# First-layer attention units: the reciprocals of the softmax sums fetched from HBM as a tenth row beside the nine taps' weights

## The chip, the core and the metric

The kernel runs on one core of one Trainium2 chip. The core has five engines that work side by side, each through its own instructions in order: TensorE (PE, matmuls; PEld is its loading of weights), VectorE (DVE), ScalarE (ACT), GpSimd (POOL) and SyncE (SP), whose queue issues the DMAs here. The metric is device time in microseconds (us) for one execution; the time of a kernel is the median of its runs.

## The reference, cut to what matters

The network has four layers; the change is in the first, an attention of 8 heads of 64 channels over 64 x 64 positions, for two images. Each position attends to its own 3 x 3 neighbourhood (nine "local" keys) and to 256 pooled keys, with one softmax over both; learned weights are added to the local part after the softmax.

```python
attn_local = jnp.einsum('bhnd,bhndk->bhnk', q_scaled, k_local)
...
attn = jax.nn.softmax(jnp.concatenate([attn_local, attn_pool], axis=-1), axis=-1)
a_local, a_pool = (attn[..., :ll], attn[..., ll:])
lt = jnp.einsum('bhnd,hdk->bhnk', q_norm, learnable_tokens) + learnable_bias[None] + a_local
x_local = jnp.einsum('bhnk,bhndk->bhnd', lt, v_local)
x_pool = jnp.einsum('bhnp,bhpd->bhnd', a_pool, v_pool)
xo = (x_local + x_pool).transpose(0, 2, 1, 3).reshape(B, N, C)
```

So the output at a position needs, for each head, ten numbers spread over the head's 64 channels: the reciprocal of the softmax sum, by which the pooled part is multiplied, and nine local weights, by which the nine shifted copies of the values are multiplied.

## The kernel before

Class `Local` computes this layer. The work is cut into 16 units per image: four chunks of 128 channels (two heads) by four pieces of 1024 positions. Channels lie on the 128 partitions. `run` goes through iterations; in each, several units are in the making at different stages, written as generators that take turns (`in_turn`): the projections and norms of later units, the tap products and sums of the next unit (`tap_products`, `tap_sums`), the attention of this one (`attend`), and the weighing of the one before (`weigh`). The framework schedules the result: it fixes an order of instructions for each engine ahead of the run, which is not always the order in which they are written, and adds the waits between engines. So what stands next to what on an engine can change in places where the code was not touched.

The steps by line:

- `tap_products` (L2126, VectorE): for tap k of 9, queries times shifted keys, 128 x 1024, into one of three buffers (product k goes to buffer k mod 3). `tap_sums` (L2139, TensorE): sums these over the 64 channels of each head; two matmuls (one for each half of 512 positions) per tap, 18 per unit, each of 32 output rows, all into one bank "tap". ScalarE's exponential (L2154) of that bank is the tile `el`: rows 2k and 2k+1 of each group of 32 belong to tap k, and the rows from 18 on have weights of zero, so there `el` is exp(0) = 1.
- `attend`: scores against the pooled keys (L2171), exponentials (L2175), values (L2181) into `out`, GpSimd's additions of the exponentials (L2186), the softmax sums in the layout of `el` (L2193, L2197), their reciprocals (L2218) in `recip`. Then `el` is multiplied by `recip` and the learned part is added (L2221, L2222; it is zero in the rows from 18 on), and `el` is written to HBM as `rows` (L2225).
- `fetch_tap` (L2235): one row of `rows` is read back for each head and written to all of the head's 64 partitions; two DMAs fill one 128 x 1024 tap tile. There are three tap tiles, taken in turn.
- `weigh`: the reciprocals are spread over the partitions by two TensorE matmuls (L2248, two rows of `recip` by a matrix of zeros and ones, into two banks), and VectorE multiplies `out` by them (L2251). Then for each tap k: ScalarE copies the tap tile into two PSUM banks (L2258), VectorE multiplies the shifted values by them, back into the tap tile (L2261), GpSimd adds the tile to `out` (L2265), and the tile is free for the fetch of tap k + 3. At the end `out` is stored to HBM as `yd` (L2271), from where `output` (L1966) reads it for the last projection.

Other lines that stand between these on the engines: L133 (the projections' matmuls), L2036, L2043, L2064, L2078 (the norms' matmuls), L2050 to L2058 (small VectorE steps of the norms), L2086 (the norms' multiplication), L2099 (learned part), L2183 (copy of the values), L1983 (loads of projection weights).

PSUM banks called "mm" come from a pool of five, given out in turn in the order in which the code asks: whoever takes a bank waits for the last reader of the tile that stood in it five requests before. The banks of L2248 and of L2258 are taken from this pool, like those of L133, L2171 and L2181.

Of the kernel before, what the change touches and what calls it, by code (L numbers as in the profile page):

```python
# [11 lines left out]
ALU = mybir.AluOpType  # L12
# [3 lines left out]
P = 128  # L16
# [4 lines left out]
TB = 512  # L21
# [3 lines left out]
HD = 64  # L25
# [16 lines left out]
def bcast(ap, axis, n):  # L42

    a = ap.unsqueeze(axis)
    shape = list(a.shape)
    shape[axis] = n
    return a.to_broadcast(shape)
# [10 lines left out]
class General:  # L58
# [130 lines left out]
    def layer0(self, X, Y, sp_scale, tokT, d):  # L189
        tc, nc, vec = self.tc, self.nc, self.vec  # L190
        with tc.tile_pool(name="l0", bufs=1) as sp:
# [7 lines left out]
            with tc.tile_pool(name="l0b", bufs=2) as wp, \  # L199
                    tc.tile_pool(name="l0s", bufs=2, space=PSUM) as pps, \  # L200
                    tc.tile_pool(name="l0m", bufs=3, space=PSUM) as pp, \
                    tc.tile_pool(name="l0o", bufs=1, space=PSUM) as ppo:
                taps = wp.tile([18, 9, P], F32, name="taps", bufs=1)
                nc.sync.dma_start(taps, d["taps"])
                steps = []
                for cc in range(KC):
                    steps += self.local_chunk(X, Y, cc, xs, nmean, rstd, sp_scale, tokT, taps, d,
                                              wp, pps, pp, ppo)
                in_turn(steps[0][0]())
                for i, (_, attend) in enumerate(steps):  # L210
                    ahead = [steps[i + 1][0]()] if i + 1 < len(steps) else []
                    in_turn(attend(), *ahead)
# [63 lines left out]
    def local_chunk(self, X, Y, cc, xs, nmean, rstd, sp_scale, tokT, taps, d, wp, pps, pp, ppo):  # L276
# [137 lines left out]
        def attend(blk):  # L414
# [48 lines left out]
            nc.vector.tensor_tensor(Y[:, cc, blk * TB:(blk + 1) * TB], acc, psO, ALU.add)  # L463

        return [(lambda b=b: prepare(b), lambda b=b: attend(b)) for b in range(NB)]


# [1225 lines left out]
class Local:  # L1693
# [464 lines left out]
    def attend(self, u):  # L2158

        nc = self.nc  # L2160
        cc = u // self.UN
        qs, el = self.qs[u % 3], self.el[u]
        out = self.att()
        prob = {}
        self.out[u] = out
        heads = [slice(h * HD, (h + 1) * HD) for h in range(2)]

        def exponentials(j, k2):
            pS = [self.bank() for _ in range(2)]
            for h, c in enumerate(heads):  # L2170
                nc.tensor.matmul(pS[h], self.kp[c, cc, k2 * P:(k2 + 1) * P],  # L2171
                                 qs[c, j * TB:(j + 1) * TB], start=True, stop=True)
            prob[j, k2] = [self.prob() for _ in range(2)]
            for h in range(2):
                nc.scalar.activation(prob[j, k2][h], pS[h], AF.Exp)  # L2175

        def values(j):
            psO = self.bank()
            for k2 in range(2):
                for h, c in enumerate(heads):  # L2180
                    nc.tensor.matmul(psO[c, :], self.vp[:, k2, cc * P + h * HD:][:, :HD],  # L2181
                                     prob[j, k2][h], start=(k2 == 0), stop=(k2 == 1))
            nc.scalar.copy(out[:, j * TB:(j + 1) * TB], psO)  # L2183
            dst = prob[1, 1] if j else self.halves
            for h in range(2):
                nc.gpsimd.tensor_tensor(dst[h], prob[j, 0][h], prob[j, 1][h], ALU.add)  # L2186

        def sums():
            psD = self.bank()
            blocks = [slice(j * HD, (j + 1) * HD) for j in range(2)]  # L2190
            for h in range(2):
                for j, b in enumerate(blocks):
                    nc.tensor.matmul(psD[b, :], self.cst[:, C_EVEN + h:C_EVEN + h + HD],  # L2193
                                     (prob[1, 1] if j else self.halves)[h], start=(h == 0),
                                     stop=False)
            for b in blocks:
                nc.tensor.matmul(psD[b, :], self.cst[b, C_SD:C_SD + HD], el[b, :], start=False,  # L2197
                                 stop=True)
            return psD

        exponentials(0, 0)
        yield
        exponentials(0, 1)
        yield
        values(0)
        yield
        exponentials(1, 0)
        yield
        exponentials(1, 1)
        yield  # L2210
        values(1)
        yield
        yield
        psD = sums()

        for i in range(2):
            part = slice(i * TB // 2, (i + 1) * TB // 2)
            nc.vector.reciprocal(self.recip[:, part], psD[:, part])  # L2218
        yield
        el = self.el.pop(u)  # L2220
        nc.vector.tensor_tensor(el, el, self.recip, ALU.mult)  # L2221
        nc.vector.tensor_tensor(el, el, self.lt.pop(u), ALU.add)  # L2222
        self.spread = self.rows()
        for j in range(2):
            nc.sync.dma_start(self.spread[:, j * TB:(j + 1) * TB], el[j * HD:(j + 1) * HD, :])  # L2225
        self.fetch_tap(0)
        yield
        self.fetch_tap(1)
        yield

    def fetch_tap(self, k):

        at = 32 * (k % 2) + 2 * k
        for h in range(2):
            self.nc.sync.dma_start(self.taps[k % 3][h * HD:(h + 1) * HD, :],  # L2235
                                   bcast(self.spread[at + h], 0, HD))

    def weigh(self, u):

        nc = self.nc  # L2240
        cc, y0 = u // self.UN, u % self.UN * self.UY
        out, R = self.out.pop(u), self.recip
        self.fetch_tap(2)
        yield
        banks = [self.bank() for _ in range(2)]
        for j, ps in enumerate(banks):
            q = slice(64 * j, 64 * j + 2)
            nc.tensor.matmul(ps, self.cst[q, C_ROW:C_ROW + P], R[q, :], start=True, stop=True)  # L2248
        for j, ps in enumerate(banks):
            o = out[:, j * TB:(j + 1) * TB]  # L2250
            nc.vector.tensor_tensor(o, o, ps, ALU.mult)  # L2251
        for k in range(9):
            dy, dx = divmod(k, 3)
            parts = [self.taps[k % 3][:, j * TB:(j + 1) * TB] for j in range(2)]

            banks = [self.bank() for _ in range(2)]
            for ps, part in zip(banks, parts):
                nc.scalar.copy(ps, part)  # L2258
            for j, (ps, part) in enumerate(zip(banks, parts)):
                y = y0 + dy + j * self.UY // 2  # L2260
                nc.vector.tensor_tensor(  # L2261
                    part.rearrange("p (y x) -> p y x", x=W),
                    self.vx[:, y:y + self.UY // 2, dx:dx + W],
                    ps.rearrange("p (y x) -> p y x", x=W), ALU.mult)
            nc.gpsimd.tensor_tensor(out, out, self.taps[k % 3], ALU.add)  # L2265
            if k + 3 < 9:
                self.fetch_tap(k + 3)
            if k < 8:
                yield
        lo = u % self.UN * self.UT  # L2270
        nc.sync.dma_start(self.yd[:, cc, lo:lo + self.UT], out)  # L2271
        yield
# [161 lines left out]
```

## Time and profile before

| | us |
|---|---|
| median of 9 runs | 5500.97 |
| lowest, highest | 5495.19, 5508.07 |
| the profiled execution: time | 5499.75 |
| the profiled execution: span from first to last instruction | 5497.9 |
| loop of units, first image | about 346 to 1112 |
| loop of units, second image | about 3070 to 3836 |

In the 766 us of each loop, TensorE is busy for 745 us, VectorE for 529, GpSimd for 415, ScalarE for 376, and the mean granted clock is 0.99. The starts of L2248 in the first image are 361.68, 407.66, 453.52 and so on to 866.33, then 906.44, 946.11, 1000.73 and 1041.15: eleven equal steps, and then units in which less is projected and the output is computed beside them.

How to read it: "busy" is the time in which an engine executes; an engine that waits is idle. Each fp32 matmul of the code is two records of MATMUL in the profile. In a timeline line stand the start, the duration, the engine, the line of the code, the operation, output and input tiles (`late` is a tile from which `out`, `el`, `recip` and the exponentials are cut; `big` holds the keys, values, queries and two of the three tap tiles), shapes, and in brackets how long the engine had been idle and on what it waited last. A matmul's end is modelled, so the start of the next one tells better how long it held the engine.

### The profile page before, as it was taken

The numbers are of one execution on the slowest core, as the hardware profiler recorded it, in microseconds if no ns is written. First come the engines' busy times: TensorE is split into PE (matmuls) and PEld (weight loads), VectorE is DVE, ScalarE is ACT, GpSimd is POOL, SyncE is SP. The second block draws the span as 40 slices with busy tenths as digits, with TensorE's granted clock in tenths as the row PEclk, the third lists the DMA queues.
The fourth block names the chain that finished last, engine by engine and source line by source line (L and its number), as shares of the span: only waits on it lengthen the run. The fifth ranks groups of instructions, "written<-read, shape, count | busy, mean of one in ns | idle before, by whom it ended". The sixth has DMA issues, their size and how long they took to land. (4 is left out here: it accounts for less than half of the span.)

```text
span 5497.9 us, 51908 instructions
## 1 busy us (share of the span) xinstructions
PE 5220.4 (95%) x19291; PEld 2259.9 (41%) x19291; DVE 3063.7 (56%) x3804; ACT 1798.5 (33%) x3441; POOL 1802.5 (33%) x1198
## 2 busy tenths in 40 slices
PE   7899999999988899999998999999999889999999
PEld 4333332554333444544343333335543334445443
DVE  3256667645679533544432666666456894334444
ACT  1245555233212233212212555542432222332221
POOL 0025556401310045434400355553013001554443
PEclk9899999999989999999998999999999899999999
DMA  3024445500000000201010344455000000000000
GB/s 140 0 58 127 127 125 155 149 18 24 1 2 0 1 0 1 77 20 35 31 52 0 83 125 127 125 151 147 1 23 1 2 0 1 1 8 16 16 16 24
DMA packets 103354, 276.37 MB, mean 50 GB/s; under 512 B 15090, under 2 KB 28146, under 8 KB 101044
## 3 DMA queue, kind: packets, MB, share of 16 engines
q1 hardware_dynamic: 103092, 272.97, 17.4%
q8 instruction: 154, 2.52, 0.2%
q14 instruction: 108, 0.88, 0.1%
HBM read 224.68 MB, written 48.23 MB: 50 GB/s over the span
## 5 line engine op out<-in xcount | busy, mean ns | idle before, releaser
L133 PE MATMUL mm<-big,w 128*128 128x512 f32 x2560 | 1193.3, 610 | 5.2 <-DVE late L2218 5.1
L133 PEld LDWEIGHTS mm<-big,w 128*128 128x128 f32 x2560 | 467.8, 192 | 699.2 <-issue 598.4
L2265 POOL TENSOR_TENSOR late<-late,big 128x1024 f32<-128x1024 f32 x192 | 454.7, 2368 | 307.3 <-DVE big L2261 305.0
L1265 POOL TENSOR_TENSOR total<-prob 128x512 f32<-128x512 f32 x128 | 159.6, 1269 | 757.4 <-ACT prob L1262 757.4
L1617 POOL TENSOR_SCALAR qf_sum<-qf,ksum_ratio 128x512 f32<-128x512 f32 x128 | 198.9, 1562 | 552.6 <-ACT qf L1667 351.3
L1182 PE MATMUL acc<-big,dg 128*128 128x512 f32 x704 | 319.9, 612 | 58.3 <-DVE big L697 25.5
L1438 POOL TENSOR_TENSOR big<-big 128x512 f32<-128x512 f32 x224 | 277.3, 1271 | 235.4 <-ACT big L1429 235.4
L2186 POOL TENSOR_TENSOR late<-late 128x512 f32<-128x512 f32 x128 | 160.7, 1277 | 510.6 <-ACT late L2175 485.3
L1642 DVE RECIPROCAL k<-psD 128x512 f32<-128x512 f32 x64 | 214.9, 3357 | 185.0 <-PE psD L1639 185.0
L697 DVE TENSOR_TENSOR big<-big 128x3968 f32<-128x3968 f32 x72 | 308.9, 4290 | 6.9 <-DVE big L697 0.9
L2261 DVE TENSOR_TENSOR big<-big,mm 128x512 f32<-128x512 f32 x384 | 254.5, 680 | 77.6 <-ACT mm L2258 74.7
L1429 ACT ACTIVATE big<-mm,ed 128x256 f32<-128x256 f32 x512 | 193.8, 488 | 276.6 <-DVE top L1425 248.8
L2258 ACT COPY mm<-big 128x512 f32<-128x512 f32 x384 | 221.4, 594 | 154.3 <-DMA big<-rows 111.3
L1363 PE MATMUL mm<-proj,k 64*128 64x256 f32 x2048 | 265.3, 391 | 0.9 <-ACT k L1330 0.9
L1282 DVE RECIPROCAL recip<-psD 128x512 f32<-128x512 f32 x64 | 214.9, 3358 | 87.2 <-PE psD L1279 87.2
L2126 DVE TENSOR_TENSOR prod<-qs,big 128x1024 f32<-128x1024 f32 x192 | 230.9, 1218 | 44.5 <-PE tap L2139 42.8
L1262 ACT ACTIVATE prob<-mm 128x512 f32<-128x512 f32 x256 | 132.0, 605 | 364.5 <-PE mm L1259 359.3
L1584 DVE TENSOR_REDUCE tops<-mm 128x2 f32<-128x512 f32 x256 | 159.4, 681 | 163.4 <-PE mm L1363 163.3
L2265 POOL TENSOR_TENSOR late<-late,tap 128x1024 f32<-128x1024 f32 x96 | 226.6, 2360 | 62.5 <-DVE tap L2261 45.0
L1363 PEld LDWEIGHTS mm<-proj,k 64*128 64x128 f32 x2048 | 207.6, 188 | 95.1 <-issue 78.7
L133 PE MATMUL mm<-big,big 128*128 128x512 f32 x512 | 238.0, 627 | 0.0
L1648 PE MATMUL mm<-k,w 128*128 128x512 f32 x512 | 235.6, 602 | 0.0
(369 smaller groups left out, 8384.4 us busy)
## 6 DMA issues: line engine op xcount, KB each, us to landing
big<-rows SPq DMA_DIRECT2D x384, 256.0 KB, 4.1
tap<-rows SPq DMA_DIRECT2D x192, 256.0 KB, 4.2
yd<-late SPq DMA_DIRECT2D x32, 512.0 KB, 4.2
out<-big SPq DMA_DIRECT2D x64, 256.0 KB, 2.0
big<-in_W_kv SPq DMA_DIRECT2D x8, 1024.0 KB, 6.6
rows<-late SPq DMA_DIRECT2D x64, 128.0 KB, 2.4
big<-yd SPq DMA_DIRECT2D x16, 512.0 KB, 4.2
big<-in_x SPq DMA_DIRECT2D x4, 2048.0 KB, 7.9
```

The lines of the kernel that those rows point to most:

```text
L133: self.nc.tensor.matmul(ps, w[:, kc, :], X[:, kc, blk * TB:(blk + 1) * TB], start=(kc == 0), stop=(kc == KC - 1))
L697: nc.vector.tensor_tensor(o, a, b, ALU.max)
L1182: nc.tensor.matmul(accs[b], dg, src[:, b * TB:(b + 1) * TB], start=(j == 0), stop=(j == 6))
L1282: nc.vector.reciprocal(r, psD)
L1363: nc.tensor.matmul(pS[h][i][:, t, :], k[lo:lo + HD, tok:tok + P], proj[lo:lo + HD, :], start=True, stop=True)
L1438: nc.gpsimd.tensor_tensor(a, a, part, ALU.add)
L1642: nc.vector.reciprocal(qs[:, cc, :], psD)
L1648: nc.tensor.matmul(ps, self.wo[:, kc, oc * P:(oc + 1) * P], qs[:, kc, :], start=(kc == 0), stop=(kc == KC - 1))
L2126: self.nc.vector.tensor_tensor(self.prods[k % 3].rearrange("p (y x) -> p y x", x=W), qs, self.kx[:, y + dy:y + dy + self.UY, dx:dx + W], A ...
L2258: nc.scalar.copy(ps, part)
L2261: nc.vector.tensor_tensor(part.rearrange("p (y x) -> p y x", x=W), self.vx[:, y:y + self.UY // 2, dx:dx + W], ps.rearrange("p (y x) -> p y ...
L2265: nc.gpsimd.tensor_tensor(out, out, self.taps[k % 3], ALU.add)
```

## The change

The rows 20 and 21 of `el` hold 1 before they are multiplied by `recip`, and the reciprocals of the two heads' sums after. The changed kernel fetches these two rows like a tap's, as item 0 of ten; taps become the items 1 to 9. The matmuls of L2248 are left out, and `out` is multiplied by banks into which ScalarE copies the fetched tile. Item 0 needs no addition by GpSimd, so its tap tile is free once it is copied. The three tap tiles are taken in turn by the number 10 u + i. Items 0 and 1 are treated in the same step of the generator, so the number of steps of `weigh` is as before.

```diff
-        self.fetch_tap(0)
+        self.fetch_tap(u, 0)
         yield
-        self.fetch_tap(1)
+        self.fetch_tap(u, 1)
         yield
 
-    def fetch_tap(self, k):
+    def fetch_tap(self, u, i):
-        at = 32 * (k % 2) + 2 * k
+        at = 32 * ((i - 1) % 2) + 2 * (i - 1) if i else 20
+        t = self.taps[(10 * u + i) % 3]
         for h in range(2):
-            self.nc.sync.dma_start(self.taps[k % 3][h * HD:(h + 1) * HD, :],
-                                   bcast(self.spread[at + h], 0, HD))
+            self.nc.sync.dma_start(t[h * HD:(h + 1) * HD, :], bcast(self.spread[at + h], 0, HD))
 
     def weigh(self, u):
-        out, R = self.out.pop(u), self.recip
-        self.fetch_tap(2)
+        out = self.out.pop(u)
+        self.fetch_tap(u, 2)
         yield
-        banks = [self.bank() for _ in range(2)]
-        for j, ps in enumerate(banks):
-            q = slice(64 * j, 64 * j + 2)
-            nc.tensor.matmul(ps, self.cst[q, C_ROW:C_ROW + P], R[q, :], start=True, stop=True)
-        for j, ps in enumerate(banks):
-            o = out[:, j * TB:(j + 1) * TB]
-            nc.vector.tensor_tensor(o, o, ps, ALU.mult)
-        for k in range(9):
+        for i in range(10):
+            t = self.taps[(10 * u + i) % 3]
+            parts = [t[:, j * TB:(j + 1) * TB] for j in range(2)]
             banks = [self.bank() for _ in range(2)]
             for ps, part in zip(banks, parts):
                 nc.scalar.copy(ps, part)
+            dy, dx = divmod(i - 1, 3)
             for j, (ps, part) in enumerate(zip(banks, parts)):
+                if i == 0:
+                    o = out[:, j * TB:(j + 1) * TB]
+                    nc.vector.tensor_tensor(o, o, ps, ALU.mult)
+                    continue
                 y = y0 + dy + j * self.UY // 2
...
-            nc.gpsimd.tensor_tensor(out, out, self.taps[k % 3], ALU.add)
-            if k + 3 < 9:
-                self.fetch_tap(k + 3)
-            if k < 8:
+            if i:
+                nc.gpsimd.tensor_tensor(out, out, t, ALU.add)
+            if i + 3 < 10:
+                self.fetch_tap(u, i + 3)
+            if 0 < i < 9:
                 yield
```

In the changed kernel the fetches are line L2237, the copies L2252, the multiplication of `out` L2257 and the taps' multiplications L2260; GpSimd's addition is still L2265 and the store L2271.

## The prediction

> **What bounds the kernel now.** First the page's table of busy time: TensorE is busy nearly all of the span, no other engine much over half.
>
> ```profile
> PE 5220.4 (95%) x19291; PEld 2259.9 (41%) x19291; DVE 3063.7 (56%) x3804; ACT 1798.5 (33%) x3441; POOL 1802.5 (33%) x1198
> ```
>
> Then the stage of the change by windows (columns: us; busy us and count of PE, PEld, DVE, ACT, POOL; granted clock; DMA share; GB/s). The loop of first-layer units runs from 346 to 1112 us, and in the second image from 3070 to 3836.
>
> ```profile
> 600.00:700.00 100.00, 99.75 (x367) 31.82 (x366) 69.81 (x114) 57.63 (x101) 57.36 (x29) 1.00 0.49 130
> ```
>
> TensorE has no gap and full clock there, so each microsecond of matmul is worth a microsecond, as long as the other engines stay ahead of it. I then read one unit in the timeline of TensorE; L2171 to the next L2171 at the same place is 45.86 us (591.09 to 636.95 on L2248), eleven times per image.
>
> ```profile
> 635.89 1.13 PE L2171 MATMUL mm<-big,kp 64*128 64x512 f32 x4
> 636.95 1.13 PE L2248 MATMUL mm<-late,cst 2*128 2x512 f32 x4
> 638.19 0.66 PE L2043 MATMUL mm<-cst,n_rows 128*128 128x128 f32 x4
> 638.85 1.94 PE L2181 MATMUL mm<-late,vp 128*64 128x512 f32 x8
> ...
> 642.77 1.04 PE L2139 MATMUL tap<-prod,cst 128*32 128x512 f32 x2
> 643.75 3.70 PE L133 MATMUL mm<-big,w 128*128 128x512 f32 x8
> 647.38 1.13 PE L2171 MATMUL mm<-big,kp 64*128 64x512 f32 x4
> ...
> 649.44 0.66 PE L2064 MATMUL mm<-cst,wide 128*128 128x128 f32 x4
> ```
>
> The pair of L2248 that goes away holds TensorE from 636.95 to 638.19: 1.24 us. L2139 are the 18 tap sums of a unit; they stand here in six groups, of 4, 1 and 4 ahead of L2064 (13.55 us after the first line) and 3, 5 and 1 behind it. Up to four run side by side, so a group of 1 costs as much as one of 4: 1.00, 0.98, 1.00, then 0.99, 1.82 and 0.97 (from the starts 607.09 to 608.08, 619.27 to 621.97 less 0.88 for L2099, 625.60 to 626.57), together 6.76 us.
>
> Last VectorE and ScalarE in the same unit:
>
> ```profile
> 642.93 1.08 ACT L2175 ACTIVATE late<-mm 128x512 f32<-128x512 f32 x2 [0.84 <-PE mm L2171]
> 643.90 0.61 ACT L2258 COPY mm<-tap 128x512 f32<-128x512 f32 x1
> ...
> 643.24 0.68 DVE L2261 TENSOR_TENSOR tap<-big,mm 128x512 f32<-128x512 f32 x1
> 643.83 0.19 DVE L2055 TENSOR_TENSOR mm<-mm,roots 128x32 f32<-128x32 f32 x1
> 643.93 1.22 DVE L2126 TENSOR_TENSOR prod<-qs,big 128x1024 f32<-128x1024 f32 x1
> 645.06 0.19 DVE L2056 TENSOR_TENSOR mm<-mm,roots 128x32 f32<-128x32 f32 x1
> ```
>
> Start to start a weighing multiply takes 0.60, a tap product 1.13, a small step 0.10, or 0.23 behind the step that it needs. The products (L2126) feed TensorE's sums; the multiplies (L2261) wait for copies, and these for DMAs, on the same in-order engine.
>
> **The change, part by part.** Removed per unit: the pair L2248, 1.24 us of the engine that bounds. Added: two DMA issues (0.54 us each on SP), two ScalarE copies (1.11 us for a pair). VectorE's two multiplies L2251 stay, as L2257. ScalarE is busy 58 us in 100 and SP's queue mostly idle, so their time lies beside TensorE; what counts is what they make late.
>
> DMAs: the reciprocals' row is fetched first, as item 0, and its fetch now stands behind the store of the unit before (L2271), which waits for the last POOL add. In before the first two fetches left at 624.04, the store at 628.01. That is 38.0 us into its unit, whose zero (the L2171 ahead of L2248) is 45.86 before 635.89. L2064 and with it POOL's adds come some 2 us later (below), so the first fetch leaves at about 40.3, and with the 4.9 us from first issue to copy that the row below shows, or some 5.9 in that burst (the third fetch beside the store landed 5.4 after its issue, median), it is there at 45.2 to 46.2. The copy that uses it stands 0.7 us into the next unit, at 47.0. I take no cost; without that cover ScalarE's exponentials (L2175) and then L2181 wait.
>
> ```profile
> 602.49 1.08 SPq L2235 DMA_DIRECT2D tap<-rows  x2
> ...
> 607.37 1.11 ACT L2258 COPY mm<-tap 128x512 f32<-128x512 f32 x2 [0.61 <-DMA tap<-rows]
> ```
>
> Order: the scheduler re-sorted the engines, and this is where I see the cost. In the changed program TensorE's sums stand in groups of 5 and 3, then 8 (products 4 to 7) ahead of L2064, and 2 behind. That is 1.85 + 0.99 + 1.88 + 0.97 = 5.69 us, 1.07 less than before. With L2248 TensorE's work falls by 2.31 us per unit. But products 0 to 7 are now wanted ahead of L2064, where before the sums of 5 to 8 and half of those of 4 came behind it.
>
> Counted from the L2171 that stands at 635.89 (zero): L2171 0, sums 1.06, L2043 2.91, L2181 3.57, sums 5.44, L2171 6.43, L133 7.49, L2171 11.12, sums 12.18; L2064 could start at 14.06. VectorE: the exponentials of the L2171 at 6.43 start 1.21 later (641.72 to 642.93), the copy of item 3 (tap 2) 0.97 behind them, at 8.61, its multiply 0.7 later, at 9.32. In order follow: multiply 0.60, small 0.10, multiply 0.60, small 0.10, product 5 1.13, small 0.10, product 6 1.13, three small 0.57, multiply of item 4 0.60, two small 0.33, product 7 1.23: 6.49, so product 7 ends at 15.81. Item 4's copy is no later: its fetch follows POOL's first add (5.2 + 2.4 = 7.6), its data are there at 12.5, its multiply stands at 13.55. So TensorE takes the last sums at 15.87 and L2064 at 16.84: 2.78 us late. The rest of the unit was 45.86 - 13.55 = 32.31; its three groups of sums (3.78) become one (0.97): 29.50. New unit: 46.34, 0.48 more than before. Twenty-two units: +10.6 us.
>
> Bounds of this wait, which no row shows: if VectorE's idle 1.3 us ahead of 9.32 vanished, the unit would be 45.04 (-0.82, -18 us in all); if all of it were hidden, -2.31, -51 us. I take 2.78, since it is the sum of rows.
>
> The clock: the wait leaves TensorE idle for 1.8 us between half-filled groups. The windows behind such a wait (L2171 at 912.69, idle 1.41 us) show the granted clock at half for some 6.8 us:
>
> ```profile
> 912.69 3.03 PE L2171 MATMUL mm<-big,kp 64*128 64x512 f32 x4 [1.41 <-DVE big L2261]
> ...
> 914.00:916.00 2.00, 2.00 (x3) 0.32 (x3) 2.00 (x5) 1.28 (x3) 1.92 (x2) 0.50 0.03 7
> 916.00:918.00 2.00, 2.00 (x3) 0.50 (x2) 2.00 (x5) 0.90 (x2) 1.50 (x1) 0.50 0.81 211
> ```
>
> The pooling stage's waits of 1.72 us between dense matmuls (1705.84) kept 1.00; the 2.93 us at 956.60 cost about 3.4 us at half. So from 0 to 3.4 us lost per unit (0 to 75 in all). I take a fall in one unit of three, 3.4 us at half, 1.7 lost: 22 / 3 x 1.7 = +12.5 us. The Trainium skill ("TensorE: Matmul & The Clock Gate", section "HAM oscillation — how this bites in real kernels") has it that idle gaps matter only above about 3.4 us. By that rule the term would be 0 and the forecast 5517; the row at 912.69 speaks against it, and decides.
>
> The ends of the loops, per image: in the next-to-last iterations 14 sums stand together ahead of L2181, so the output matmuls that began at 957.58 wait for product 6 (ends 957.68) and then two L2181/L2139 groups, to about 962.5: +4.9, less three groups that fall out later, 3.0. Two L2248 fall out, -2.1. TensorE waits at 1046.35 and 1050.27 for banks; these now wait for the reciprocals' DMA, which leaves at 1043.9 rather than 1041.13: +2.8. Together +2.6, for two images +5.2.
>
> **Sum.** 10.6 + 12.5 + 5.2 = +28.3 on the span of 5497.9: 5526; with the 1.9 us around it 5528, and the profiled run was 1.2 under the median: **5529 us**.
>
> **Rivals.** (1) Product 7 is in time, because ScalarE and VectorE run further ahead than I count; then TensorE's saving is kept: 5501 - 51 + 5 = 5455, faster. For it: TensorE is the bound and does 2.3 us less per unit; against it: VectorE has 6.49 us of work in a fixed order behind 9.32. It decides once product 7 ends by 13.0, 2.8 us earlier than I count. (2) Part of the wait is hidden, and saving and wait cancel: -18 + 5 and no fall of the clock gives 5488, the middle of the case is 5498. (3) The half clock comes in every unit for 6.8 us, as at 912.69: 5501 + 10.6 + 5.2 + 75 = 5592.
>
> **How the numbers follow.** Forecast 0.50 (own range 5512 to 5565), rival 3 0.12, rival 2 0.13, rival 1 0.25. 0.2% is 11 us, about what a measurement of this kernel tells from no change: faster 0.25, same 0.13, slower 0.62. The range reaches from near rival 1 to near rival 3: 5460 to 5585.
>
> **What would show it.** L2139 ahead of L2064 with about 1.8 us of idle time that ends on VectorE's L2126, in each of 22 units; starts of L2064 46.3 us apart or more; a granted clock under 1.00 in the windows of 400 to 860. If L2064 comes 43.5 us apart, the step on product 7 was wrong. If TensorE waits at L2181 or L2171 instead, the DMA behind the store was it.

## The result and the profile after

The changed kernel takes 5521.48 us (median of 10 runs, 5516.27 to 5527.78), the kernel before 5499.11 (33 runs, 5490.84 to 5510.82); the ratio is 1.0039, with a 95% interval of 1.0031 to 1.0048. It is slower by some 22 us. The profiled execution has a span of 5525.4 us.

In the page's table of busy time TensorE does 28 us less work than before (5220.4), and the span is 27.5 us longer:

```profile
PE 5192.7 (94%) x19163; PEld 2262.0 (41%) x19163; DVE 3053.9 (55%) x3804; ACT 1831.0 (33%) x3505; POOL 1805.9 (33%) x1198
```

In the windows, 600 to 700 us (columns as before), TensorE now has 5 us of gaps where it had none, still at full clock:

```profile
600.00:700.00 100.00, 95.04 (x345) 30.76 (x345) 69.40 (x116) 58.43 (x103) 56.71 (x28) 1.00 0.56 144
```

The timeline of TensorE in one unit shows the gap:

```profile
598.07 1.13 PE L2171 MATMUL mm<-big,kp 64*128 64x512 f32 x4
...
603.82 1.06 PE L2139 MATMUL tap<-prod,cst 128*32 128x512 f32 x8
604.80 1.05 PE L2139 MATMUL tap<-big,cst 128*32 128x512 f32 x4
607.50 1.05 PE L2139 MATMUL tap<-prod,cst 128*32 128x512 f32 x4 [1.65 <-DVE prod L2126]
608.49 0.65 PE L2064 MATMUL mm<-cst,wide 128*128 128x128 f32 x4
```

and VectorE's what it waits for:

```profile
600.90 0.69 DVE L2260 TENSOR_TENSOR tap<-big,mm 128x512 f32<-128x512 f32 x1 [1.26 <-ACT mm L2252]
...
606.24 1.22 DVE L2126 TENSOR_TENSOR prod<-qs,big 128x1024 f32<-128x1024 f32 x1
607.37 0.18 DVE L2058 SCALAR_TENSOR_TENSOR wide<-mm,roots 128x32 f32<-128x32 f32 x1
```

The sums of product 7 stand ahead of L2064, as in the order that the prediction read, and wait for that product in all 22 units. But the last root step (L2058), whose result `wide` is what L2064 transposes, stands behind product 7 on VectorE and ends at 607.55. So without these sums L2064 could have started only some 0.9 us earlier than 608.49. The prediction did not look at this second input.

The starts of L2064 are 46.06 us apart (45.86 before). This can't be the 22 us, so I cut each loop of units in two at the last L2064: the *head* runs from the first L2064 to the last, the *tail* from there to the first L87, the first matmul behind the loop. The rest of the span, whose code is the same, is "outside". Sums of both images in the profile, after less before: heads +1.8 us, tails +14.7, outside +11.0. In the tail of the first image the longest wait of the loop is new. TensorE before, and after:

```profile
1041.15 1.13 PE L2248 MATMUL mm<-late,cst 2*128 2x512 f32 x4
1046.35 2.10 PE L1966 MATMUL mm<-sq,big 128*128 128x512 f32 x2 [4.07 <-DVE late L2251]
1050.27 2.10 PE L1966 MATMUL mm<-sq,big 128*128 128x512 f32 x2 [1.82 <-DVE big L2261]
```

```profile
1020.57 2.11 PE L1966 MATMUL mm<-sq,big 128*128 128x512 f32 x4 [0.68 <-ACT late L2175]
...
1056.87 3.80 PE L1966 MATMUL mm<-sq,big 128*128 128x512 f32 x4 [9.92 <-DVE late L2257]
```

In the last unit the output's matmuls L1966 wait for a bank, which the multiplication of `out` by the reciprocals (L2251 before, L2257 after) frees. SP's queue, ScalarE and VectorE of the changed kernel show why it is late:

```profile
1043.84 1.11 SPq L2225 DMA_DIRECT2D rows<-late  x2
...
1046.88 2.39 SPq L2237 DMA_DIRECT2D big<-rows  x4
```

```profile
1054.91 1.11 ACT L2252 COPY mm<-big 128x512 f32<-128x512 f32 x2 [11.07 <-DMA big<-rows]
```

```profile
1055.53 1.29 DVE L2257 TENSOR_TENSOR late<-late,mm 128x512 f32<-128x512 f32 x2 [4.15 <-ACT mm L2252]
```

The reciprocals go out to HBM at 1043.84, are asked back at 1046.88, and are there for the copy at 1054.91, 11.07 us after the way through HBM began. The two fetches of this row took 6.9 and 7.4 us from issue to landing, against a median of 4.1 over the kernel. Before, the two matmuls at 1041.15 gave the reciprocals to VectorE without it. TensorE, idle for 9.92 us, comes back at half clock: four records of L1966 at 1056.87 take 3.80 us, against 2.11 for four at full clock (at 1020.57). The half clock is not new, though: in the kernel before it holds from 1043.5 to 1053.8 us, 10.2 us as here, and two records at 1046.35 take 2.10 us. New is the idle time: over the two tails TensorE is idle for 25.9 and 24.5 us, before for 16.0 and 15.1.

### The profile page after: what moved, and what is told of

Read it like the earlier page. It is cut to its first block, busy times and chain, and to the rows that moved or that the text cites. A ratio compares the mean times of both kernels' runs of the same rounds, so it can differ in the third digit from the quotient of the medians.

```text
span 5525.4 us, 51859 instructions
## 1 busy us (share of the span) xinstructions
PE 5192.7 (94%) x19163; PEld 2262.0 (41%) x19163; DVE 3053.9 (55%) x3804; ACT 1831.0 (33%) x3505; POOL 1805.9 (33%) x1198
## 5 line engine op out<-in xcount | busy, mean ns | idle before, releaser
L2265 POOL TENSOR_TENSOR late<-late,big 128x1024 f32<-128x1024 f32 x192 | 455.0, 2370 | 267.5 <-DVE big L2260 252.1
L2260 DVE TENSOR_TENSOR big<-big,mm 128x512 f32<-128x512 f32 x384 | 254.4, 681 | 77.7 <-ACT mm L2252 73.3
L2252 ACT COPY mm<-big 128x512 f32<-128x512 f32 x428 | 244.0, 596 | 151.8 <-DMA big<-rows 121.3
L2265 POOL TENSOR_TENSOR late<-late,tap 128x1024 f32<-128x1024 f32 x96 | 227.5, 2370 | 141.6 <-DVE tap L2260 134.0
L2139 PE MATMUL tap<-prod,cst 128*32 128x512 f32 x768 | 198.7, 601 | 40.3 <-DVE prod L2126 39.8
```

The source lines that it names most:

```text
L2260: nc.vector.tensor_tensor(part.rearrange("p (y x) -> p y x", x=W), self.vx[:, y:y + self.UY // 2, dx:dx + W], ps.rearrange("p (y x) -> p y ...
L2265: nc.gpsimd.tensor_tensor(out, out, t, ALU.add)
```

## The experiments

All the numbers are from one profile of each kernel (period: median distance of L2064 in 22 units; head, tail: mean of the two images, us) and from times of this kernel and the kernel before on one chip. "With gap" and "in turn" are explained at the runs on the tail.

| kernel | ratio to before (95%) | period | head | tail | outside |
|---|---|---|---|---|---|
| before | | 45.86 | 698.6 | 187.1 | 3726.5 |
| before, again | 1.0006 (0.9995 to 1.0018) | 45.86 | 698.3 | 184.3 | 3721.7 |
| changed | 1.0039 (1.0031 to 1.0048) | 46.06 | 699.6 | 194.4 | 3737.4 |
| e1 sums of 7 behind | 1.0039 (1.0025 to 1.0053) | 45.25 | 699.8 | 192.8 | 3725.6 |
| e2 roots first | 1.0033 (1.0021 to 1.0044) | 45.72 | 696.2 | 193.9 | 3734.1 |
| e3 and sums grouped | 1.0034 (1.0023 to 1.0044) | 45.75 | 694.4 | 195.3 | 3737.4 |
| e5 roots before third tap | 1.0022 (1.0013 to 1.0031) | 45.41 | 691.5 | 195.5 | 3734.6 |
| e4 last unit by matmul, with gap | 1.0049 (1.0035 to 1.0063) | 46.06 | 699.8 | 195.0 | 3720.7 |
| e6 last four by matmul, with gap | 1.0096 (1.0081 to 1.0110) | 46.06 | 708.2 | 201.0 | 3738.2 |
| e7 e5 and e6 | 1.0069 (1.0055 to 1.0083) | 45.47 | 697.8 | 201.1 | 3733.7 |
| e8 last four, in turn | 1.0027 (1.0016 to 1.0038) | 46.06 | 701.0 | 185.4 | 3730.2 |
| e9 last unit, in turn | 1.0019 (1.0010 to 1.0028) | 46.06 | 699.0 | 187.4 | 3721.1 |
| e10 e5 and e8 | 0.9984 (0.9974 to 0.9994) | 45.49 | 688.5 | 186.9 | 3722.5 |
| e11 tenth item and matmul | 1.0089 (1.0074 to 1.0105) | 46.62 | 708.7 | 191.8 | 3735.2 |

**Is it product 7 that makes L2064 late?** (e1) The edit queues the sums of products 7 and 8 behind the last transpose on TensorE (`issue_after` fixes an order on one engine and adds no other wait).

```diff
+            self.turned = nc.tensor.transpose(ps[:, t * P:(t + 1) * P], self.wide[:, t, :],
+                                              self.net.ident).ins
...
+                behind = self.turned if k >= 7 else None
+                with self.net.tc.issue_after(behind) if behind else nullcontext():
```

> The changed kernel; on TensorE the tap sums of products 7 and 8 (L2139) are kept behind the last transpose L2064, nothing else is reordered. Theory A (the prediction's step: L2064 is late because the sums of product 7 stand ahead of it): the wait of 1.65 us on product 7 goes, L2064 starts at 605.8 rather than 608.5 of its unit, the steady period falls from 46.05 to about 43.5 us, and the time by 22 x 2.6 = 57 us, to about 5464. Theory B (VectorE itself has been put in another order: product 7 stands ahead of the last root step L2058, which ends at 607.55 and which L2064 needs as well): L2064 then waits for L2058 instead, starts at about 607.6, the period falls by 0.6 to 0.9 us only, to about 45.3, and the time to about 5505.

Theory B: the period is 45.25, 0.8 less than the changed kernel's, and L2064 waits for L2058 (one line further down in this kernel: L2059; L2181 is L2185):

```profile
465.60 0.63 PE L2065 MATMUL mm<-cst,wide 128*128 128x128 f32 x4 [1.85 <-DVE wide L2059]
466.16 3.36 PE L2185 MATMUL mm<-late,vp 128*64 128x512 f32 x8
...
512.49 0.63 PE L2065 MATMUL mm<-cst,wide 128*128 128x128 f32 x4 [1.85 <-DVE wide L2059]
513.05 1.94 PE L2185 MATMUL mm<-late,vp 128*64 128x512 f32 x8
```

The time did not fall to the 5505 us that goes with it, though (median 5516.68), and these lines show why: the same wait of 1.85 us is followed once by L2185 at 3.36 us and once at 1.94. In this profile's clock record all changes of the granted clock lie a whole number of stretches of 3.41 us apart. The windows below lie on this grid: the one that ends within L2185, and the next, for both units:

```profile
463.12:466.53 3.41, 1.56 (x10) 0.62 (x8) 3.38 (x8) 1.90 (x5) 0.35 (x1) 1.00 0.58 161
466.53:469.94 3.41, 3.41 (x10) 0.98 (x8) 1.84 (x3) 1.17 (x3) 2.31 (x2) 0.50 0.03 10
...
510.90:514.32 3.42, 1.83 (x10) 0.90 (x12) 3.40 (x6) 1.67 (x3) 1.25 (x1) 1.00 0.57 147
514.32:517.73 3.41, 3.41 (x12) 1.17 (x9) 2.60 (x5) 1.60 (x3) 3.41 (x3) 1.00 0.28 80
```

The first wait lies whole in one window (TensorE busy for 1.56 of 3.41 us), and the next window has half clock; the second wait began before the window did (busy for 1.83), and the clock stayed. All 22 units sort this way: the clock fell behind the 8 windows with 1.84 or 1.85 us of idle time, and behind none with 1.76 or less. So where on the grid a wait fell decided here. Seven of the 8 units took 46.89 (1.65 more), one 50.87. That is 7 x 1.65 + 5.6 = 17 us, which cancels 22 x 0.8.

**VectorE in the order of before** (e2, e3, e5). The roots are put ahead of products 6 to 8 (e2), and with it the sums of products 4 to 8 behind L2064 (e3).

```diff
+            self.rooted = nc.vector.scalar_tensor_tensor(dst, a, 1.5, y, ALU.add, ALU.mult).ins
...
+            behind = self.rooted if k >= 6 else None
+            with self.net.tc.issue_after(behind) if behind else nullcontext():
+                self.nc.vector.tensor_tensor(self.prods[k % 3]...
```

> The changed kernel; on VectorE the tap products 6, 7 and 8 (L2126) are kept behind the last root step L2058, as they stand in the kernel before. TensorE's order follows: sums of 5, 3 and 1 ahead of L2064, of 3, 5 and 1 behind it. Theory B: no wait ahead of L2064; the unit is the one of before without L2248 and with groups that take 0.84 us more (7.6 against 6.76): about 45.45 us, 0.4 under the kernel before; with the ends unchanged (+14 over before) the time is about 5499 - 9 + 14 = 5504. Theory C (the tenth fetch and the two copies cost the steady unit about what L2248 gave, whatever the order): the period stays at 46.0 or above and the time at about 5520.

> As the run with the roots first, and on TensorE the sums of products 4 to 8 behind L2064: groups of 5 and 3 ahead, 4, 5 and 1 behind (6.61 us). Theory B: no wait ahead of L2064, period about 44.5 us, 1.55 under the changed kernel, so 22 x 1.55 = 34 us less: about 5487, faster than the kernel before by 0.2%. Theory A says the same of the period. Theory C: period 45.9 or above, the saving turns up as waits at L2171, L2181 or L2064 for copies; time 5515 or above.

Both periods are 45.7, whatever the grouping: under the kernel before, but above the 45.45 and 44.5 of theory B, and the times (5517.97 and 5515.33 us) are theory C's. In e2 hardly a wait is left at L2064 (0.19 us at the median); in e3 the unit takes 1.2 us more than TensorE's work. TensorE, VectorE and ScalarE of e3 (L2065 is L2064, L2266 the taps' multiply, L2181 the exponentials, L2258 the copies):

```profile
597.57 0.66 PE L2065 MATMUL mm<-cst,wide 128*128 128x128 f32 x4 [1.17 <-DVE wide L2059]
```

```profile
593.41 0.69 DVE L2266 TENSOR_TENSOR tap<-big,mm 128x512 f32<-128x512 f32 x1 [1.26 <-ACT mm L2258]
```

```profile
591.80 1.08 ACT L2181 ACTIVATE late<-mm 128x512 f32<-128x512 f32 x2 [1.46 <-PE mm L2177]
592.77 1.11 ACT L2258 COPY mm<-tap 128x512 f32<-128x512 f32 x2
```

Read from the bottom: the exponentials wait for TensorE, the copy of item 3 stands behind them, its multiply waits for the copy, and the root steps stand behind the multiply. The next run takes the multiplies of items 3 to 9 out of the roots' way:

```diff
+                behind = self.rooted if i >= 3 else None
+                with self.net.tc.issue_after(behind) if behind else nullcontext():
+                    nc.vector.tensor_tensor(part.rearrange("p (y x) -> p y x", x=W), ...
```

> As the run with the roots first and the sums grouped, and on VectorE the multiplies (the second operation of an item) of items 3 to 9 are kept behind the last root step too. Theory D (the wait left at L2064 comes from item 3: its multiply stands ahead of the root steps, waits for ScalarE's copy, and this stands behind the exponentials L2175 that wait for TensorE's L2171; the tenth item pushed every tap one place later, so that item 3 came to stand there): no wait at L2064 and a steady period of about 44.4 us instead of 45.65, so about 27 us less than that run: 5488. Rival E (ten items through three tap tiles need 45.6 us per unit by themselves: fetch, copy, multiply, add): the wait moves to another place, the period stays at 45.5 or above and the time at about 5515.

The wait at L2064 goes, but the period is 45.41, a quarter of the way from 45.75 to 44.4, and the time 5507.05 us. The wait has moved to the values' matmul (L2181 of the kernel before, here L2187; L2181 is again the exponentials here). ScalarE, and TensorE:

```profile
514.08 0.59 ACT L2258 COPY mm<-big 128x512 f32<-128x512 f32 x1 [0.58 <-DMA big<-rows]
514.60 1.08 ACT L2181 ACTIVATE late<-mm 128x512 f32<-128x512 f32 x2
```

```profile
515.25 1.94 PE L2187 MATMUL mm<-late,vp 128*64 128x512 f32 x8 [0.68 <-ACT late L2181]
```

ScalarE waits for a tap's DMA with the exponentials behind it; in the 22 units TensorE waits there for 0.6 us and at L2078 (here L2080) for ScalarE's copy `n_rows` for 0.45 (medians). So theory D was right about L2064 and wrong about the period, and the wait moved as rival E said. That ten items through three tap tiles need 45.4 us by themselves is not shown: neither a fourth tile nor the exponentials ahead of that copy was tried.

**The tail** (e4, e6 to e10). Units from a number on get their reciprocals by the two matmuls L2248 and fetch nine rows, as before: the last unit, the last four, and the last four together with e5.

```diff
+        first = int(u >= 12)
+        self.fetch_tap(u, first + 2)
         yield
+        if first:
+            banks = [self.bank() for _ in range(2)]
+            for j, ps in enumerate(banks):
+                q = slice(64 * j, 64 * j + 2)
+                nc.tensor.matmul(ps, self.cst[q, C_ROW:C_ROW + P], self.recip[q, :], start=True,
+                                 stop=True)
...
+        for i in range(first, 10):
```

> The changed kernel; only in the last of 16 units of each image the reciprocals are spread by the two matmuls L2248 as before, and nine rows are fetched. Theory of the ends: the output's wait of 9.92 us on L2257 near the end of each loop goes back to the 5.9 us (4.07 + 1.82) of the kernel before, and the matmuls behind it to full clock sooner: about -6 us per image, -12 in all, time about 5510; the steady period stays 46.05. Rival: the end is late only because the loop is late, and the wait is bounded by the last taps' fetches: then the wait moves to L2260 and the time stays at 5521.

> The changed kernel; the reciprocals of the units 12 to 15 of each image are spread by the matmuls L2248, with nine rows fetched, as in the kernel before; units 0 to 11 as changed. Theory F (the tail, from the last L2064 to the first L87 behind the loop, is 194.5 us rather than 187 because each of the last four units has a tenth item in it): tail about 187 to 188, steady period 46.05, time about 5507. Rival G (the tail is longer because the order of sums and banks in the last iterations was changed by what comes before; as with the last unit alone by matmul): tail 193 or above, time about 5521.

> Both edits together: units 12 to 15 by matmul, and in all units the roots ahead of products 6 to 8 and of the multiplies of items 3 to 9, the sums of products 4 to 8 behind L2064. Theories D and F: period 44.4, tail about 188, time about 5473, 0.5% under the kernel before. If only D holds 5488, if only F holds about 5500, if neither about 5515.

All three missed their expectations (medians 5523.55, 5547.39 and 5534.51 us), and a flaw of my edit has to do with it: the tiles were still taken by 10 u + i, so each of these units skipped one of the three tap tiles, and its first fetch went into a tile that was freed later. The same edits with the items counted without a gap:

```diff
+    def item(self, u, i):
+        return 10 * u + i - max(0, u - 12 + 1)
...
-        t = self.taps[(10 * u + i) % 3]
+        t = self.taps[self.item(u, i) % 3]
```

> As the run with the last four units by matmul, but the tap tiles are counted on without a gap (that run skipped one tile of the three at each of these units, so that a unit's first fetches had to wait for the adds of the last items of the unit before). Theory F (a tenth item in each of the last four units makes the tail 7.5 us longer): tail (last L2064 to the first L87 behind the loop) 187 to 189 us, steady period 46.05, time about 5507. Rival G (the order of sums and banks in the last iterations is what costs): tail 193 or above, time 5521 or above.

> As the run with the last unit by matmul, tap tiles counted on without a gap. Theory F: the wait of 9.92 us on L2257 falls to about the 5.9 us of before, the waits of the units 12 to 14 (2.0, 2.6, 3.9) stay: tail about 191, time about 5514. Rival G: tail 194 or above, time 5521.

Theory F holds in e8 (tail 185.4, median 5510.28 us), and e9 gives more than it said: the last unit alone brings the tail from 194.4 to 187.4, about the value of before (median 5508.40). TensorE at the place of the 9.92 us wait in e9 (L2255 is L2248):

```profile
1033.35 1.13 PE L2255 MATMUL mm<-late,cst 2*128 2x512 f32 x4
1038.56 2.10 PE L1966 MATMUL mm<-sq,big 128*128 128x512 f32 x2 [4.08 <-DVE late L2259]
1041.14 2.10 PE L1966 MATMUL mm<-sq,big 128*128 128x512 f32 x2 [0.47 <-DVE big L2274]
```

This wait is again that of the kernel before, and so is the clock, at half for 10.2 us from 1035.9. The skipped tile, an accident, shows how much hangs on the order: between e6 and e8 the code differs only in which tile an item takes, and the medians are 5547.39 and 5510.28 (on two chips; ratios 1.0096 and 1.0027). How the 37 us come about (the waits, or what the scheduler made of them) I did not follow further.

> The run with the roots ahead of the third tap (steady period 45.4 us) with units 12 to 15 by matmul and the tiles counted on without a gap. Theories D and F: period 45.4, tail about 188, time about 5507 - 14 = 5493, level with the kernel before (5496). Without F 5507.

This version beats both kernels: 5485.62 us against 5496.35 for the kernel before in the same comparison, ratio 0.9984 (0.9974 to 0.9994). In units 0 to 11 it does without the matmuls, with the order of VectorE and TensorE mended; in the last four units it keeps them. The gain is small, 0.16%. How much of it the mended order would give the kernel before was not run.

**The tenth item by itself** (e11). The row is fetched and copied, nothing reads the copies, and the reciprocals come by the matmuls.

```diff
+        for j, ps in enumerate(banks):
+            q = slice(64 * j, 64 * j + 2)
+            nc.tensor.matmul(ps, self.cst[q, C_ROW:C_ROW + P], self.recip[q, :], ...
...
                 if i == 0:
-                    o = out[:, j * TB:(j + 1) * TB]
-                    nc.vector.tensor_tensor(o, o, ps, ALU.mult)
                     continue
```

> The tenth item alone: its row is fetched and copied into banks as in the changed kernel, but nothing reads them; the reciprocals are spread by the matmuls L2248 as before. If VectorE's and ScalarE's order with ten items sets the steady period (theories B and D), L2248 fits partly into the wait on product 7: period about 46.3 to 46.5, not 46.05 + 1.24 = 47.3; tail 194 or above; time 5525 to 5535. If TensorE's own work sets it: period 47.3, time about 5550. If the tenth item costs nothing: the time of before, 5496.

The period is 46.62, near the first of the three cases, 0.56 over the changed kernel and not 1.24: part of L2248 fits into the wait on product 7, which is shorter here. TensorE of e11:

```profile
611.51 1.05 PE L2139 MATMUL tap<-prod,cst 128*32 128x512 f32 x4 [0.84 <-DVE prod L2126]
```

The time is 5546.27, more than expected. In heads and tails the tenth item costs 29.5 us against the first profile of before, and taking the matmuls away on top of it gives 12.9 back: the changed kernel's loops add up to 16.6.

**A control** (the kernel before, once more). What is outside the loops had been between 3721 and 3738 us, which is as much as the effects sought.

> The kernel before, unchanged, as a control: a second profiled execution of it. Of its span 1771 us lie in the two loops of units (first L2064 to the first L87 behind the loop) and 3726.5 outside; in the changed kernels so far the part outside, whose code is the same, was between 3721 and 3738 us, and their medians stand some 9 us higher than the loops' share explains. Theory H (the part outside scatters with the granted clock from execution to execution, and one profile of the kernel before says little of it): loops 1771 to 1772 again, the part outside anywhere from 3720 to 3738, ratio 1.000. Theory K (something outside the loops is slower in all changed kernels): loops and part outside as in the first profile, within 2 us.

The loops were 6.3 us shorter than in the first profile (2.8 us of a tail, on average), the part outside 4.8. That the loops would agree within a microsecond did not come true. Of the part outside, each theory has a piece. Ahead of the first loop the two profiles differ by 6.9 us (225.8 and 218.9), and the other kernels lie between 215.2 and 229.8, as theory H has it. But between the two loops both take 1838.8 us, and each of the twelve other kernels takes 2.0 to 11.7 more, as theory K has it. Windows of that part (columns as before) in the kernel before, the same again, and the changed kernel:

```profile
1111.96:2950.71 1838.75, 1745.45 (x6778) 807.82 (x6778) 959.78 (x995) 481.90 (x1000) 481.40 (x389) 0.97 0.06 20
```

```profile
1100.70:2939.57 1838.87, 1745.67 (x6777) 808.05 (x6778) 959.86 (x995) 481.92 (x1000) 481.48 (x389) 0.97 0.05 20
```

```profile
1121.34:2968.45 1847.11, 1755.26 (x6778) 815.46 (x6778) 959.78 (x995) 482.46 (x1000) 482.02 (x389) 0.96 0.06 20
```

TensorE's matmuls are the same in the same order; in the changed kernel it takes 10 us more for them, because the granted clock is at half for 149 us rather than 125. Why it falls more often there is open. Differences of a tail under about 3 us can't be read from single profiles; the 7 us of the tails can: with the fetch in the last unit (the changed kernel, e1 to e3 and e5) ten tails lie between 190.9 and 196.4, without it and with tiles in turn (before twice, e8 to e10) ten lie between 183.5 and 187.9. The two of e11, where the row is fetched and copied but not used, are 191.6 and 191.9.

## Why the prediction was right or wrong

The time, its sign and the place of the steady wait were right; that the sum came so near is luck. Of the 28.3 us, 23.1 were for the steady units and their clock, where the heads cost 1.8; the ends cost 14.7 instead of 5.2; and 11.0 of the profile's 27.5 lie outside the loops, for which the prediction had no term.

- **Steady unit, +0.48 x 22 = +10.6.** The wait was as told: TensorE waits 1.65 us for product 7 (1.8 predicted), L2064 starts 16.75 us after the unit's zero (16.84), product 7 ends at 15.7 (15.81). The rest of the unit took 29.30 rather than 29.50, so the unit is 46.05 and not 46.34: +0.20 instead of +0.48. With the first and the last iterations of the heads, which lost 3.1 and gained some 4 per image, the heads cost 1.8 us together. What the step left out is that the order of the root steps makes L2064 late as well; e1 shows that moving the sums alone gains 0.8 us of a unit.
- **The clock, +12.5.** Wrong for this kernel: the windows show 1.00 from 360 to 860 us and from 3110 to 3600. The rule of the Trainium skill that the prediction weighed and set aside would have given the right term here. e1 shows that the rule is not safe either: 1.85 us was enough there, 8 times in 22. The single row at 912.69, after which the prediction took one unit in three, did not carry over: 1.65 us in these units was too little, wherever on the grid it fell.
- **Tenth item's DMA and copies, no cost in the steady state.** Right as the kernel stands; e3 and e5 show how near it is. Once the wait on product 7 is gone, waits that end on ScalarE's copies and then on the fetches keep the unit at 45.4 to 45.7, so rival 1's 43.55 us (45.86 - 2.31) and 5455 were not to be had by the orders tried.
- **Ends, +5.2 for both images.** Right in kind, off in size: the tails cost 14.7. The term that was mis-sized is the banks that wait for the reciprocals' DMA, +2.8 per image. I took only the delay of the fetch's start; the wait is for the whole way, 3.04 us from the store to the fetch and 8.03 from the fetch to the copy. e9 prices it at 7.0 per image; the half clock behind it was there before too.

Heads and tails explain 16.6 of the 22 us against the first profile of before and 22.9 against the second. Of the 11.0 us outside them in the profiles, 8.3 lie between the two loops, where the clock is at half for longer. e8 and e9 point the same way: their heads and tails add up to 1772.8 us, 1.4 and 7.7 more than in the two profiles of before, but their times are 0.27% and 0.19% above that kernel's. What in the change brings this about is not shown.

## What to carry to other kernels

Replacing an engine's work by a way through memory is free only where something hides the whole way: price it separately in the steady loop and in the last iteration, where nothing is left to hide it, and keep the short way there. A new step on two engines with much slack can still cost on the one that has none, because the scheduler places everything else anew: look at all inputs of each instruction that ends up late, not at the last one alone. And when a wait is taken away, ask at once which is next in line; here there were three, of 1.65, 1.17 and 0.68 us in the units shown, and taking away the first gained 0.8 us of a unit, the second 0.3.

## What the runs showed of the hardware

- The granted clock: 19 waits of 1.65 to 1.68 us between half-filled groups (the changed kernel) left it at 1.00 each time; 19 waits of 1.84 and 1.85 in the same place (e1) were followed by half clock 8 times, for 3.4 us (once 10.2), and three of 1.48 never. The clock changed only on a grid of 3.41 us, and what decided in e1 was the idle time within one window of that grid: with 1.84 us the next window had half clock each time, with 1.76 never. Idle time alone is not the measure, since 1.41 us at 912.69 in the kernel before was enough. The Trainium skill ("TensorE: Matmul & The Clock Gate", section "HAM oscillation — how this bites in real kernels") puts the limit at about 3.4 us of idle time; e1 does not agree with that.
- A fetch of 256 KB from HBM takes 4.1 us from issue to landing at the median of the changed kernel; in the tail's burst (1040 to 1062 us, DMA engines busy for 0.79 of the time) the median of ten such fetches is 6.9.
